# Four-layer graph attention on one core: a planner's rules and durations changed, and layer 3's transfers of half blocks joined

## The chip, the core and the metric

The kernel runs on one core of a Trainium2 chip. What counts is device time in microseconds, from the first to the last instruction of one launch; the runs before gave 2981.0, 2978.83 and 2983.35, median 2981.0. The core has five engines that run their own instruction streams: TensorE (PE in the profile; its weight loads are PEld), VectorE (DVE), ScalarE (ACT), GpSimd (POOL) and SyncE (SP), which here issues nearly all DMA transfers.

## What is computed

128 graphs of 64 nodes, 512 features each, go through four attention layers with a residual. Each layer normalizes, applies a ReLU, attends over the nodes that the adjacency allows, and adds the result to its input:

```python
# layers 0 to 3
h = jnp.maximum(_layernorm(x, axis=-1), 0.0)
x = x + _Ll_gnn_ref(h, adj, ...)

# layers 0 and 2: 4 heads of 64
q, k, v = split_heads(x @ Wq), split_heads(x @ Wk), split_heads(x @ Wv)
sim = jnp.where(adjacency_mask[:, None], jnp.einsum('bhid,bhjd->bhij', q, k) * scale, neg)
out = jnp.einsum('bhij,bhjd->bhid', jax.nn.softmax(sim, axis=-1), v)
return out.transpose(0, 2, 1, 3).reshape(B, N, INNER) @ Wo + bo

# layer 1: the same with 8 heads, and a layernorm of its own (gamma, beta) ahead of w_qkv

# layer 3: 8 heads of 64
m = embs @ map_w.T + map_b
n = sem / norm                                  # m by heads, each row over its length
cos_adj = einsum('bhsd,bhtd->bhst', n, n) * (~sm) > 0.1
q, k = m @ q_w.T + q_b, m @ k_w.T + k_b         # by heads
p_attn = softmax(where(sm, NEG, q k^T / 8)) * keep
adj = cos_adj * p_attn
Ax = einsum('hbst,hbtd->hbsd', adj, embs @ gcn_map_w.T + gcn_map_b)   # by heads
out = relu((Ax @ gcn_W.T) / (adj.sum(-1) + 1.0))
```

Everything is in float32.

## The kernel before

The 8192 rows are cut into 16 groups of 512 rows (`TB` = 4 blocks of 128 rows, two graphs each). A step (l, s) is layer l on group s; 64 steps run through, layer by layer, and neighbouring steps overlap.

**A step.** `loads` brings the group's rows in (xin, two transfers of 512 KB, issued on SP); `layernorms` takes statistics on VectorE (L390, L392), a power on POOL (L397), one more small operation on VectorE (L399) and the normalization with ReLU on ScalarE (L406). `transposes` turns the rows by TensorE into ptr (L477; L454 in layer 1) and copies them with ScalarE to hT (L482). The projections follow; then `front` makes the scores (L824, PSUM tile sc), masks them (L835), takes the maximum (L840), subtracts (L843), exponentiates on ScalarE (L846), sums (L849), inverts (L851) and scales on POOL (L853, tile E). `attention` transposes E (L864, copied by L868 to pt), multiplies with v (L983, tile po), and projects back with a residual that `residuals` has loaded to xres; `store` writes the rows to HBM, where the next layer reads them. In layer 3 `last` multiplies E with the values (L1118, tile po3, two blocks of 128 rows per transposed E), `finish` divides, adds the residual (L1029 to L1040) and writes to the output (L1047); `last_residuals` has loaded the residual (L1019).

**A projection** is a Strassen-Winograd product (`winograd`): seven products of halves in place of eight, with sums of the operands made beforehand (`sums_of_b`: L326 on POOL, L323 on VectorE; `sums_of_a` for the weights). The products are named by their PSUM banks: mA, mB, mA (with a sum of the inputs, t), mC, mA, mC, mA. Each product of a bank that still holds something unread must wait until this has been read. The readers are the methods of `Out`: `first` copies with ScalarE (L529, or L533 with a bias), `second` adds on VectorE from PSUM (L542), `add` copies with ScalarE to a spare quarter (L549) and then adds on VectorE (L553), `alone` copies the last product (1, 0) into that same quarter. `Residual` (layers 0 to 2's projections back) copies with ScalarE to u (L924) and adds on POOL (L929). v in layers 0 and 2 is a plain product (L659, bank mmv, copied by L651). PSUM banks: sc one (shared by sc, po and po3), mA two, mm two (mB, mC, mmv, mmn), ptr and ptp two.

**What sets the order.** Nothing is left to a scheduler of the compiler: each engine's instructions stand in the order in which this program emits them, and each engine works through its own in that order, waiting where data are missing. The order comes from a planner in the program. Every loop above is a generator (a stream) that yields an engine, a duration and a latency ahead of each instruction; `Order.run` keeps a clock for each engine and always lets the stream go on whose next instruction could start first; at equal starts the lower priority number wins. The readers of PSUM have number 0, `fronts` 1, `attentions` 2, `transposes` 3, `weights`, `loads` and `layernorms` 4, projections 5. A load is planned with 0.35 us on SP and 2.2 us until it has landed. `Event` is a wait within the plan; the waits on the chip are made by the tile framework from what each instruction reads and writes. `Ring` and `Bank` hand out buffers and make a stream wait in the plan until an older buffer is given back.

Of the kernel before, what the change touches and what calls it, by code (L numbers as in the profile page):

```python
# [43 lines left out]

class Event:
# [38 lines left out]


class Order:


    def __init__(self):
        self.live, self.free, self.now, self.held = [], {}, 0.0, set()  # L90

# [28 lines left out]

    def run(self):
        while self.live:
            new = [s for s in self.live if s.op is None]
            if new:
                self.step(new[0])
                continue
            s = min(self.live, key=lambda s: (s.start(self.free), s.prio))
            eng, dur, lat = s.op
            at = s.start(self.free)
            self.free[eng] = at + dur  # L130
            s.ready = at + dur + lat
            s.last = (eng, at + dur)
            self.step(s)
        assert not self.held, [where(s.gen) for s in self.held]
# [51 lines left out]

def dve(us):
    return ("dve", us, 0.1)
# [10 lines left out]
def load(us=2.2):  # L199
    return ("sp", 0.35, us)  # L200
# [3 lines left out]
def gnn_stack(ctx: ExitStack, tc: tile.TileContext, a: dict, out: bass.AP):  # L204
# [111 lines left out]
    def sums_of_b(B, T, vector=False):  # L316

        n = T.shape[2]
        for o, i0, i1 in ((T[:, 0], B(0, 1), B(0, 0)), (T[:, 1], B(1, 1), T[:, 0]),
                          (T[:, 2], B(1, 1), B(0, 1)), (T[:, 3], B(1, 0), T[:, 1])):  # L320
            if vector:
                yield dve(0.6 * n)
                nc.vector.tensor_tensor(o, i0, i1, ALU.subtract)  # L323
            else:
                yield pool(0.65 * n)
                nc.gpsimd.tensor_tensor(o, i0, i1, ALU.subtract)  # L326
# [57 lines left out]
    def scales(v):  # L384
# [13 lines left out]
        yield dve(0.2)  # L398
# [4 lines left out]
    def normalize(v, rs, func):  # L403
        for t in range(2):
            yield act(0.69)
# [11 lines left out]
    def loads(steps):  # L417
        for l, s in steps:
            if l > 0:
                yield x_done[l - 1, s]  # L420
            for half in range(2):
                v, e = yield from r_xin.new()
                loaded[l, s, half] = v, e
                yield load()
# [94 lines left out]
    class Out:  # L519
# [5 lines left out]
        def first(self, i, k, p_, read, done):  # L525
# [4 lines left out]
            else:  # L530
                for m in range(2):
                    yield act(0.45)
# [12 lines left out]
        def add(self, i, k, p_, after, read, done):  # L545
# [6 lines left out]
            yield dve(0.7)  # L552
# [3 lines left out]
        def alone(self, i, k, p_, done):  # L556
            yield from self.first(i, k, p_, done, od.event())

    def winograd(A, BT, tokens_out, out_, used, begun):

        B, T, *sums = BT

# [3 lines left out]
        def first(i, k, p_):  # L566
            read, done = ev(2)
            od.spawn(out_.first(i, k, p_, read, done), 0)
            return read, done

        def second(i, k, p_, after):
            done = od.event()
            od.spawn(out_.second(i, k, p_, after, done), 0)
            return done

        def add(i, k, p_, after):
            read, done = ev(2)
            od.spawn(out_.add(i, k, p_, after, read, done), 0)
            return read, done
# [26 lines left out]
        od.spawn(out_.alone(1, 0, p_, pe_), 0)  # L606
        od.spawn(when([c11, c12, c22, pe_], used), 0)
# [152 lines left out]
    def norms(mT, s, m_ready, ready, used):  # L760
# [30 lines left out]
        for c in range(NC):  # L791
            t, e = yield from r_u.new("nr")
            yield ("sp", 0.35, 1.0)
# [15 lines left out]
    def scores(lT, rT, npair, blocks):  # L809
# [3 lines left out]
        for b, t in enumerate(blocks):  # L813
            for ch in range(nch):
                j = ch * nb + b
                yield pe(0.29)
# [55 lines left out]
    def masks(l, s):  # L872
# [3 lines left out]
        yield load()  # L876
# [22 lines left out]
    def residuals(l, s, w_there, got):  # L899
        yield w_there  # L900
        for k in range(2):
            xr, xe = yield from r_xres.new()
            yield load()
# [8 lines left out]
    class Residual(Out):  # L912
# [26 lines left out]
        def alone(self, i, k, p_, done):  # L939
            return self.second(i, k, p_, None, done)  # L940

    def store(l, s, done, got, evs):
# [3 lines left out]
        for k in range(2):  # L946
            xr, xe = got[k]
            yield load()
# [10 lines left out]
    def attention(l, s):  # L959
# [8 lines left out]
        for u, blocks in enumerate(units):  # L968
# [3 lines left out]
            for b, t in enumerate(blocks):  # L972
                for ch in range(nch):
                    j = ch * per + b
                    yield pe(0.29)
# [32 lines left out]
    def last_residuals(s, got):  # L1008
        for t in range(TB):
            if t % 2 == 0:  # L1010
                v2, e2 = yield from r_xres.new()
            v = v2[:, t % 2, :]
            e = e2 if t % 2 else None
            xr = v.rearrange("p (g e) -> p g e", g=2)
            for s2 in range(2):
                for g in range(2):
                    ch = s2 ^ g
                    yield load()
                    nc.sync.dma_start(  # L1019
                        xr[s2 * N:(s2 + 1) * N, g, :],  # L1020
                        x_of(3, s)[t * P + g * N:t * P + (g + 1) * N, ch * 256:(ch + 1) * 256])
            got[t] = (v, xr, e)
            got["e", t].set()

    def finish(s, t, po, poe, got):
# [17 lines left out]
        for s2 in range(2):  # L1043
            for g in range(2):
                ch = s2 ^ g
                yield load()
                nc.sync.dma_start(out[row + g * N:row + (g + 1) * N, ch * 256:(ch + 1) * 256],  # L1047
                                  xr[s2 * N:(s2 + 1) * N, g, :])
# [48 lines left out]
    def last(s):  # L1097
# [3 lines left out]
        for u in range(2):  # L1101
# [3 lines left out]
            for b, t in enumerate(blocks):  # L1105

                po, poe = yield from r_sc.new("po3")
                for i in range(4):
                    yield pe(0.15)
# [90 lines left out]
```

## Time and profile before

The profiled execution took 2978.9 us on the core, at a granted TensorE clock of 0.996.

| | busy us | share of the span | instructions |
|---|---|---|---|
| TensorE, products | 2910.6 | 98% | 27176 |
| TensorE, weight loads | 2468.1 | 83% | 27176 |
| VectorE | 1727.3 | 58% | 2748 |
| POOL | 1465.2 | 49% | 1144 |
| ScalarE | 1336.6 | 45% | 2361 |

A product of 128 x 256 floats is two instructions in the profile, whose starts are about 0.216 us apart when nothing is missing (eight of them take some 1.73 us). By layer, from the busy time in stretches: layer 0 ends near 490 us, layer 1 near 1440, layer 2 near 1960, and layer 3's last step lies behind 2900. DMA is busy at 24.3% on the queue of SP.

In a line of the waits there stand: the waiting engine, tile and line, the releaser, the idle time in total, how many times, and the longest. In a line of the timeline: start and duration in us, engine, line, operation, output and input, shapes, how many, and in brackets the idle time of the engine before it and what ended it.

### The profile page before, as it was taken

The numbers are of one execution on the slowest core, as the hardware profiler recorded it, in microseconds if no ns is written. First come the engines' busy times: TensorE is split into PE (matmuls) and PEld (weight loads), VectorE is DVE, ScalarE is ACT, GpSimd is POOL, SyncE is SP. The second block draws the span as 40 slices with busy tenths as digits, with TensorE's granted clock in tenths as the row PEclk, the third lists the DMA queues.
The fourth block names the chain that finished last, engine by engine and source line by source line (L and its number), as shares of the span: only waits on it lengthen the run. The fifth ranks groups of instructions, "written<-read, shape, count | busy, mean of one in ns | idle before, by whom it ended". The sixth has DMA issues, their size and how long they took to land.

```text
span 2978.9 us, 63888 instructions
## 1 busy us (share of the span) xinstructions
PE 2910.6 (98%) x27176; PEld 2468.1 (83%) x27176; DVE 1727.3 (58%) x2748; ACT 1336.6 (45%) x2361; POOL 1465.2 (49%) x1144
## 2 busy tenths in 40 slices
PE   8999999999999999999999999999999999999997
PEld 6888888888888888888888888887888787888876
DVE  5665566664554555445456556556666666665566
ACT  4444445544444444433444444454444444444442
POOL 6666667444344334335566566663344343344332
PEclk9999999999999999999999999999999999999998
DMA  5323333211112112113233332422232222222212
GB/s 163 116 88 123 95 101 126 67 62 66 48 45 73 59 44 73 59 44 98 94 114 104 102 116 88 138 82 64 72 90 83 63 62 66 70 85 71 52 48 62
DMA packets 162957, 244.05 MB, mean 82 GB/s; under 512 B 17392, under 2 KB 69616, under 8 KB 162672
## 3 DMA queue, kind: packets, MB, share of 16 engines
q1 hardware_dynamic: 149760, 226.56, 24.3%
q10 hardware_dynamic: 12912, 13.42, 1.4%
q8 instruction: 213, 3.49, 0.5%
q14 instruction: 72, 0.59, 0.1%
HBM read 168.60 MB, written 71.30 MB: 81 GB/s over the span
## 4 chain that ended last, share of the span: by engine, by line
PE 85%; DVE 6%; ACT 4%; DMA 2%; POOL 2%; issue 1%; SPq 0%; DVEq 0%; ACTq 0%; POOLq 0%
PE mA L516 37%; PE mC L516 18%; PE mB L516 10%; PE sc L824 4%; PE mmv L659 4%; PE ptp L864 3%; PE ptr L477 3%; PE po L983 2%; ACT E L846 1%; PE po L1118 1%; DVE E L843 1%; DVE sc L835 1%; DVE mx L840 1%; PE mmn L773 1%; PE ptr L454 1%
## 5 line engine op out<-in xcount | busy, mean ns | idle before, releaser
L853 POOL TENSOR_TENSOR E<-E,sm 128x1024 f32<-128x1024 f32 x96 | 186.3, 1941 | 424.2 <-DVE sm L851 298.7
L390 DVE BATCH_NORM_STATS2 st<-xin 128x6 f32<-128x512 f32 x320 | 215.6, 674 | 260.2 <-DMA xin<-x 206.9
L929 POOL TENSOR_TENSOR xres<-xres,u 128x512 f32<-128x512 f32 x192 | 243.4, 1268 | 250.0 <-ACT u L924 245.0
L908 POOL TENSOR_TENSOR xres<-xres,u 128x512 f32<-128x512 f32 x192 | 257.7, 1365 | 219.5 <-DMA xres<-x 99.6
L406 ACT ACTIVATE xin<-xin,rs 128x512 f32<-128x512 f32 x320 | 243.7, 808 | 110.9 <-DVE rs L399 110.7
L397 POOL TENSOR_TENSOR rs<-rs,mhalf 128x2 f32<-128x2 f32 x160 | 118.4, 740 | 276.9 <-DVE rs L395 270.3
L659 PE MATMUL mmv<-w_vo,hT 128*128 128x256 f32 x1024 | 233.4, 380 | 0.9 <-DVE xres L542 0.9
L659 PEld LDWEIGHTS mmv<-w_vo,hT 128*128 128x128 f32 x1024 | 193.5, 190 | 29.0 <-DVE xres L542 2.6
L326 POOL TENSOR_TENSOR t<-hT 128x512 f32<-128x512 f32 x128 | 178.3, 1393 | 73.2 <-ACT hT L482 39.0
L326 POOL TENSOR_TENSOR t<-hT,t 128x512 f32<-128x512 f32 x128 | 172.3, 1346 | 50.5 <-ACT hT L459 46.6
L399 DVE SCALAR_TENSOR_TENSOR rs<-mv,rs 128x2 f32<-128x2 f32 x160 | 80.3, 502 | 197.7 <-POOL rs L397 197.7
L516 PE MATMUL mA<-t,w_qk 128*128 128x256 f32 x768 | 187.0, 380 | 2.8 <-ACT qk L529 2.5
L516 PE MATMUL mA<-t,w_k 128*128 128x256 f32 x768 | 182.7, 381 | 4.8 <-ACT kT L533 4.7
L516 PE MATMUL mA<-t,w_q 128*128 128x256 f32 x768 | 187.1, 379 | 0.0
L516 PEld LDWEIGHTS mA<-t,w_k 128*128 128x128 f32 x768 | 144.8, 190 | 28.2 <-ACT kT L533 8.3
L516 PEld LDWEIGHTS mA<-t,w_qk 128*128 128x128 f32 x768 | 143.1, 190 | 22.0 <-ACT qk L529 3.3
L868 ACT COPY pt<-ptp 128x512 f32<-128x512 f32 x192 | 112.7, 588 | 105.1 <-PE ptp L864 105.1
L516 PEld LDWEIGHTS mA<-t,w_q 128*128 128x128 f32 x768 | 143.1, 190 | 18.1
L849 DVE TENSOR_REDUCE sm<-E 128x16 f32<-128x1024 f32 x96 | 116.4, 1212 | 69.5 <-ACT E L846 69.5
L757 POOL TENSOR_TENSOR v<-v,gcn_row 128x512 f32<-128x512 f32 x64 | 81.4, 1305 | 150.4 <-ACT v L615 150.4
L482 ACT COPY hT<-ptr 128x512 f32<-128x512 f32 x192 | 113.7, 592 | 74.1 <-PE ptr L477 74.1
L846 ACT ACTIVATE E<-E 128x1024 f32<-128x1024 f32 x96 | 101.5, 1058 | 83.6 <-DVE E L843 83.3
(210 smaller groups left out, 6819.0 us busy)
## 6 DMA issues: line engine op xcount, KB each, us to landing
x<-xres SPq DMA_DIRECT2D x96, 512.0 KB, 3.8
xin<-x SPq DMA_DIRECT2D x96, 512.0 KB, 3.8
xres<-x SPq DMA_DIRECT2D x64, 512.0 KB, 4.2
xin<-in_x SPq DMA_DIRECT2D x32, 512.0 KB, 3.8
xres<-in_x SPq DMA_DIRECT2D x32, 512.0 KB, 4.6
u<-rs SPq DMA_DIRECT2D x128, 128.0 KB, 3.1
xres<-x SPq DMA_DIRECT2D x256, 64.0 KB, 2.3
out<-xres SPq DMA_DIRECT2D x256, 64.0 KB, 2.1
```

Of the source, the lines that this page charges most:

```text
L326: nc.gpsimd.tensor_tensor(o, i0, i1, ALU.subtract)
L390: nc.vector.bn_stats(st, v[:, t, :])
L397: nc.gpsimd.tensor_tensor(rs[:, 0, :], rs[:, 1, :], mhalf[:, :2], ALU.pow)
L406: nc.scalar.activation(v[:, t, :], v[:, t, :], func, bias=rs[:, 2, t:t + 1], scale=rs[:, 0, t:t + 1])
L516: nc.tensor.matmul(o, l, r, start=(first and m == 0 and k == 0), stop=(k == KC - 1), skip_group_check=True)
L659: nc.tensor.matmul(p_[:, 0:n], inT[:, c, t * P:(t + 1) * P], w[:, c, :], start=(c == 0), stop=(c == NC - 1))
L824: nc.tensor.matmul(S[a_ * N:(a_ + 1) * N, par, col], lT[r, c, k], rT[r, c, k], start=True, stop=True)
L846: nc.scalar.activation(E, E, AF.Exp, scale=0.125)
L849: nc.vector.tensor_reduce(sm, E, AX.X, ALU.add)
L853: nc.gpsimd.tensor_mul(E, E, sm[:, :, None].to_broadcast([P, 16, N]))
L908: nc.gpsimd.tensor_add(xr[:, t, :], xr[:, t, :], bo[l])
L929: nc.gpsimd.tensor_add(v, v, both(u))
```

## The change

Three things are changed. First, the planner: `urgent` looks, before an instruction of ScalarE or VectorE with a number above 0 is emitted, whether a stream with number 0 could start on that engine before that instruction would end (less 0.1 us), and emits this one instead. Second, durations in the plan: a switch between products on quarters of the array (`quads`: scores, po, po3) and others counts 0.085 us, and loads, normalization, sums and some others have new numbers. In `winograd`, `alone` waits in the plan until the quarter it writes has been added (c22), and `used` is set after every reader instead of after the last ones. Third, layer 3's residuals and outputs go in two transfers of 64 x 2 x 256 floats for each block of 128 rows, where it were four of 64 x 256; `by_half` builds the pattern of addresses in HBM.

```diff
+DRAIN = 0.085
...
+    def quads(self):
+        return self.op[3:] == ("quads",)
...
+    def urgent(self, s):
+
+        eng, end = s.op[0], s.start(self.free) + s.op[1] - 0.1
+        if s.prio <= 0 or eng not in ('act', 'dve'):
+            return None
+        r = [x for x in self.live if x.prio <= 0 and x.op is not None and x.op[0] == eng
+             and x.start(self.free) < end]
+        return min(r, key=lambda x: x.start(self.free), default=None)
...
             s = min(self.live, key=lambda s: (s.start(self.free), s.prio))
-            eng, dur, lat = s.op
+            s = self.urgent(s) or s
+            eng, dur, lat = s.op[:3]
             at = s.start(self.free)
+            if eng == "pe":
+                at += DRAIN * (self.quads != s.quads())
+                self.quads = s.quads()
...
 def load(us=2.2):
-    return ("sp", 0.35, us)
+    return ("sp", 0.6, us)
...
-                yield dve(0.6 * n)
+                yield dve(0.9)
...
-                yield pool(0.65 * n)
+                yield pool(1.42)
...
-        yield dve(0.2)
+        yield dve(0.45)
...
-            yield act(0.69)
+            yield act(0.81)
...
-                yield load()
+                yield load(3.9)
...
-            yield dve(0.7)
+            yield dve(0.92)
...
-        def alone(self, i, k, p_, done):
+        def alone(self, i, k, p_, after, done):
+            yield after
             yield from self.first(i, k, p_, done, od.event())
...
-        od.spawn(out_.alone(1, 0, p_, pe_), 0)
-        od.spawn(when([c11, c12, c22, pe_], used), 0)
+        od.spawn(out_.alone(1, 0, p_, c22, pe_), 0)
+        od.spawn(when([*every, pe_], used), 0)
...
-            yield ("sp", 0.35, 1.0)
+            yield ("sp", 1.3, 3.1)
...
-                yield pe(0.29)
+                yield quads(0.235)
...
-            yield load()
+            yield load(4.6)
...
     def last_residuals(s, got):
-        for t in range(TB):
-            if t % 2 == 0:
-                v2, e2 = yield from r_xres.new()
...
-            for s2 in range(2):
-                for g in range(2):
-                    ch = s2 ^ g
-                    yield load()
-                    nc.sync.dma_start(
-                        xr[s2 * N:(s2 + 1) * N, g, :],
-                        x_of(3, s)[t * P + g * N:t * P + (g + 1) * N, ch * 256:(ch + 1) * 256])
...
+        for t in range(0, TB, 2):
+            v2, e2 = yield from r_xres.new()
+            x3 = v2.rearrange("p t (g e) -> p t g e", g=2)
+            for b in range(2):
+                for s2 in range(2):
+                    yield load(2.3)
+                    nc.sync.dma_start(x3[s2 * N:(s2 + 1) * N, b],
+                                      by_half(x_of(3, s), (t + b) * P, s2))
...
+    def by_half(x, row, s2):
+
+        v = x[row:row + N, s2 * H:(s2 + 1) * H]
+        return bass.AP(tensor=v.tensor, offset=v.offset,
+                       ap=[[D, N], [N * D + (-H if s2 else H), 2], [1, H]])
...
         for s2 in range(2):
-            for g in range(2):
-                ch = s2 ^ g
-                yield load()
-                nc.sync.dma_start(out[row + g * N:row + (g + 1) * N, ch * 256:(ch + 1) * 256],
-                                  xr[s2 * N:(s2 + 1) * N, g, :])
+            yield load(2.3)
+            nc.sync.dma_start(by_half(out, row, s2), xr[s2 * N:(s2 + 1) * N])
```

## The prediction

> **What bounds the kernel now.** I read the page first: TensorE is busy almost without a break, and the chain that ended last is made of its products.
>
> ```profile
> PE 2910.6 (98%) x27176; PEld 2468.1 (83%) x27176; DVE 1727.3 (58%) x2748; ACT 1336.6 (45%) x2361; POOL 1465.2 (49%) x1144
> ...
> PE 85%; DVE 6%; ACT 4%; DMA 2%; POOL 2%; issue 1%; SPq 0%; DVEq 0%; ACTq 0%; POOLq 0%
> ```
>
> The change neither adds nor drops a product, so at the same clock (0.996) it can win only what TensorE idles: 2978.9 - 2910.6 = 68.3 us, 2.3% of the span. The second view is the list of TensorE's waits by releaser; its first nine lines hold nearly all of that.
>
> ```profile
> PE ptr L477 <- ACT xin L406: 12.9, 3, 9.7
> PE mC L516 <- ACT m L533: 8.6, 15, 0.6
> PE mC L516 <- ACT u L924: 6.2, 16, 0.5
> PE po L1118 <- DVE y L1034: 5.4, 3, 2.3
> PE po L1118 <- ACT pt L868: 5.4, 2, 5.2
> PE mmf L363 <- DVE xres L542: 4.7, 1, 4.7
> PE mA L516 <- ACT kT L533: 4.7, 4, 1.2
> PE mA L516 <- ACT qk L529: 2.5, 2, 1.4
> PE mA L516 <- ACT v L529: 1.9, 1, 1.9
> ```
>
> Nearly every line is a product that waits until ScalarE or VectorE has read its PSUM bank. Cut by layer (windows at 490, 1440, 1960 and 2900 us) the same view gives about 21 us for layer 0 (9.7 of them the first load), 4 for layer 1, 7.5 for layer 2, 16 for layer 3 and 13 for the last 79 us. Two stretches of the timeline show why. In layer 0 the Exp (L846) stands on ScalarE ahead of the copies that free the bank of mC:
>
> ```profile
> 251.68 1.06 ACT L846 ACTIVATE E<-E 128x1024 f32<-128x1024 f32 x1 [1.46 <-DVE E L843]
> 252.64 0.35 ACT L651 COPY v<-mmv 128x256 f32<-128x256 f32 x1
> 252.89 0.59 ACT L924 COPY u<-mC 128x512 f32<-128x512 f32 x1
> ...
> 253.53 1.13 PE L516 MATMUL mC<-w_vo,m 128*128 128x256 f32 x4 [0.27 <-ACT u L924]
> ```
>
> In layer 3 VectorE waits for a load (L390), behind it the addition L553, behind that on ScalarE the last copy of qT, then the first of kT, and behind this TensorE:
>
> ```profile
> 2617.20 0.69 DVE L390 BATCH_NORM_STATS2 st<-xin 128x6 f32<-128x512 f32 x1 [4.81 <-DMA xin<-x]
> ...
> 2617.81 1.34 DVE L553 TENSOR_TENSOR qT<-qT 128x512 f32<-128x512 f32 x1
> ...
> 2619.25 0.84 ACT L533 ACTIVATE qT<-mA,vecs 128x256 f32<-128x256 f32 x2 [5.79 <-DVE qT L553]
> ...
> 2620.87 1.99 PE L516 MATMUL mA<-t,w_k 128*128 128x256 f32 x8 [1.17 <-ACT kT L533]
> ```
>
> [...] through the 4.7 us of mmf no later product starts. So where a product stands decides what its wait holds up. [...] the built programs change between 64-row and 128-row products 505 times each, before and after: no gain. [...] The 32 loads here at L781 and L846 take 1283 ns, and Exp follows at once (load at 2890.30, Exp at 2891.59)[...].
>
> **The change, part by part.** I compared the order in which both built programs stand on each engine; instruction counts are equal everywhere but on SP (1042 before, 786 after).
>
> *Readers of PSUM first* (`urgent`). In layers 0 and 2 the Exp stands just ahead of the copy of mC in 31 of 32 steps before; after, in 2, and behind the copies in 28. The copy takes 0.59 us and the product in between, four passes on mA, spaces the two mC products by about 0.86 us: so much is hidden, and the wait of 4.2 (layer 0) + 2.0 (layer 2) = 6.2 us goes. I take -6.2; ends -3 and -10 (the view leaves out gaps under 0.15 us). VectorE's read of mB now precedes the masking copy (L835, 1.23 us): -0.9 us, the wait of mmv on it. In layer 3 the Exp with its table load (1.28 + 1.06 us) still stands ahead of the copy of mC in 15 of 16 steps, as before: the 8.6 us stay.
>
> *Measured durations and `alone` after c22.* The load of xin counts 3.9 + 0.6 us in the plan, in place of 2.2 + 0.35; it landed after 5.2 us in the stretch above. In 11 of layer 3's 16 steps bn_stats stood directly ahead of qT's L553; after, in none: work on po3 comes between, and SP issues the load right behind the stores of the second po3 block, some 8 us of products before bn_stats, so 5 us of landing are hidden. The new wait of `alone` holds only its own copy back in the plan; on the chip that copy already waited for L553 (same tile), so it costs nothing. I take the whole 4.7 us of kT; ends 0 and -6. Of the single waits at the start of layer 0 (2.5) and of layer 3 (2.3 of y) I take -2 together; ends +3 and -5, as the order there changes without a pattern. The 9.7 us of the first load and mmf stay: around mmf both programs have the same order, and it waits for a store and a reload.
>
> *Events of `used`.* A tile is given back in the plan when its last addition is planned, not earlier. That moves emissions, adds no instruction, and the tile framework had these waits anyway: 0.
>
> *Layer 3's transfers.* 512 issues of 64 KB (median 0.595 us each on SP, 2.3 and 2.1 us to landing) become 256 of 128 KB. If one of 128 KB costs the same issue, SP is relieved of 256 x 0.595 = 152 us, none on TensorE's path: the residuals are read many products ahead. Only at the end is a store exposed: the last addition starts at 2973.39 and takes 0.69, four issues follow, the last at 2976.0. Two fewer save 2 x 0.6 = 1.2 us. A transfer of 128 KB may land later: another of that size, the row vectors u<-rs, takes 3.1 us against 2.1. So between -1.2 and +0.1; I take -1.
>
> *What the new order costs.* Work that no product waits for directly is pushed back. The tightest such chain is in layers 0 and 2: Exp, sum (1.20), reciprocal (0.25), scaling on POOL (1.90), then TensorE's transposes.
>
> ```profile
> 256.13 1.90 POOL L853 TENSOR_TENSOR E<-E,sm 128x1024 f32<-128x1024 f32 x1
> ...
> 259.68 0.60 PE L864 MATMUL ptp<-ident,E 128*128 128x128 f32 x4
> ```
>
> Before, it had 259.68 - 258.03 = 1.65 us to spare. With Exp behind both copies (end about 253.9), it ends at 253.9 + 1.06 + 1.2 + 0.25 + 1.9 = 258.3, and with gaps of about 0.1 between engines near 258.4; the transposes come 0.27 earlier, at 259.4. So 1.0 us is left and nothing is lost, if POOL is free at 256.5: of its residual additions (1.27 each) the two ahead end by 255.4. In layer 3 sem's products are no longer interleaved with q's, which brings the two po3 products of a block to 1.7 us apart; the bank is freed in about 1.3 (0.17 + 0.20 + 0.69 and hops). For plans now packed closer to the truth I put +2 us of small waits; ends 0 and +20 (0.6 us in each of 32 steps).
>
> Sum: -6.2 - 0.9 - 4.7 - 2 - 1 + 2 = -12.8 us against the profiled span of 2978.9, so 2966. The three runs have a median of 2981.0, 2.1 above that span: 2981.0 - 12.8 = 2968.
>
> **The rivals.**
> *The waits only move.* Copies come earlier, yet the waits turn up at the next product; ScalarE and VectorE are held idle for readers that come later than planned. For it: waits of 0.3 to 0.6 us come from ordering within a product, and the plan omits table loads. Against it: at 45% and 58% both engines have room. Time: the parts above at about zero, 2975 to 2987, middle 2981. Chance 0.19.
> *The softmax chain becomes the bound* (the slower side). Place: POOL's scaling ahead of the transposes in layers 0 and 2, 32 steps. Its margin falls to 1.0 us by my sum; it decides once the chain slips more than about 1.6 us, as each 0.1 us beyond the margin costs 3.2 us. A slip of 1.7, one POOL addition of 1.3 in the way and a little more, gives 0.7 x 32 = 22, less 12.8: +10, so 2991. For it: POOL is busy 314 of 490 us in layer 0. Against it: the additions ahead of it have their data in time. Chance 0.09.
> *More goes than I count.* The single waits at the layers' seams and the short gaps go too: -25 us, 2956 or less. The 68 us bound it; without first load, mmf, mC of map and the tail's 10 us about 35 are open. Chance 0.12.
> That the transfers aren't halved is excluded by the count on SP.
>
> **How the numbers follow.** Forecast 2968 with chance 0.60 (2957 to 2975 by its own bounds). Below 2955 I leave some 0.09 of the third rival and of the bounds, above 2984 some 0.10, so the range is 2955 to 2984. About 0.2% (6 us) is what a measurement of this kernel can tell from no change. Faster by more: 0.60 + 0.12 = 0.72; within: 0.19; slower: 0.09.
>
> **What would show it.** Right: the lines of mC <- ACT u and mA <- ACT kT gone from TensorE's waits, mC <- ACT m still near 8.6, mmf near 4.7, the last out issues two fewer. Wrong: new lines of ptp or po3 behind POOL, pt or y that repeat 16 or 32 times, or a busy time of TensorE that moves by more than 5 us.

## The result and the profile after

The changed kernel takes 2969.24 us (median of 4 runs, 2967.39 to 2970.03) where the kernel before takes 2980.59 (4 runs, 2978.83 to 2983.35): a ratio of 0.996, 95% interval 0.9943 to 0.9977, or 11.4 us less. The profiled execution took 2967.7 us at the same clock of 0.996, 11.2 less than the one before.

The busy times on the page of the changed kernel:

```profile
PE 2894.8 (98%) x27176; PEld 2465.2 (83%) x27176; DVE 1755.2 (59%) x2748; ACT 1347.4 (45%) x2361; POOL 1470.5 (50%) x1144
```

TensorE's busy time fell by 15.8 us (2910.6 to 2894.8), with the same 27176 instructions. Its idle time rose: 2967.7 - 2894.8 = 72.9 us against 68.3. So the gain is not made of waits that went. The list of TensorE's waits by releaser, changed kernel (total us, times, longest):

```profile
PE ptr L501 <- ACT xin L430: 17.8, 2, 9.4
PE ptp L894 <- DVE E L1120: 15.7, 15, 1.2
PE mC L540 <- ACT m L557: 8.6, 15, 0.6
...
PE mmf L387 <- DVE xres L566: 4.1, 1, 4.1
PE po L1147 <- DVE y L1066: 2.5, 2, 1.4
PE mA L540 <- ACT kT L573: 1.5, 1, 1.5
```

(The lines moved: L516, L824, L864, L1085, L1091, L1118, L773 and L785 of before are now L540, L854, L894, L1114, L1120, L1147, L803 and L815.) The waits of mC on u (6.2 us before) and of mmv are gone, kT fell from 4.7 to 1.5, y from 5.4 to 2.5, qk and v nearly went: with the smaller ones some 20 us. In their place stand three things: ptp on E, 15.7 us where it was 0.5; the start, ptr 17.8 where it was 12.9; and the end, where from the last addition's start to the end it takes 7.5 us (2960.17 to 2967.7) where it took 5.5. With two single waits that are new or longer, by 1.1 us (po on E) and 1.4 us (mmf on bb), these bring some 24.5 us.

**Where the busy time went.** The groups of instructions by shape, norm products (mmn), before and then after; behind the bar is their busy time in us:

```profile
L773 PE MATMUL mmn<-u,sel 128*32 128x512 f32 x128 | 32.8, 605 | 0.0
```

```profile
L803 PE MATMUL mmn<-u,sel 128*32 128x512 f32 x128 | 19.3, 605 | 0.0
```

These 64 products (two instructions each) explain 13.5 of the 15.8 us. The timeline of TensorE in layer 3, before and then after, says why:

```profile
2715.13 1.04 PE L773 MATMUL mmn<-u,sel 128*32 128x512 f32 x2
2716.11 0.66 PE L864 MATMUL ptp<-ident,E 128*128 128x128 f32 x4
2716.69 1.06 PE L773 MATMUL mmn<-u,sel 128*32 128x512 f32 x6
```

```profile
2257.36 0.60 PE L894 MATMUL ptp<-ident,E 128*128 128x128 f32 x4
2257.89 1.07 PE L803 MATMUL mmn<-u,sel 128*32 128x512 f32 x8
```

One product alone takes 1.04 us, three take 1.06, four take 1.07. Each is on 32 columns of the array (128*32 in the lines), and by these times four of them run side by side, if nothing stands between them. Before, transposes stood between the first and the other three in 15 of 16 steps: 31 separate runs. After, there are 18. About 1.05 us for each run gives 32.6 and 18.9.

**The new wait of ptp.** Timeline of layer 3, changed kernel:

```profile
2269.79 1.16 PE L854 MATMUL sc<-m 64*64 64x64 f32 x64
...
2269.83 2.56 DVE L815 RECIPROCAL u<-u 128x128 f32<-128x128 f32 x3
...
2272.31 1.16 DVE L1114 SCALAR_TENSOR_TENSOR Cf<-sc,n 128x1024 uint8<-128x1024 f32 x1
...
2273.58 2.04 DVE L1120 TENSOR_TENSOR E<-E,Cf 128x1024 f32<-128x1024 f32 x1
...
2275.76 0.63 PE L894 MATMUL ptp<-ident,E 128*128 128x128 f32 x4 [1.19 <-DVE E L1120]
```

Three reciprocals of the next step's norms run on VectorE between the scores of m and Cf, the comparison that reads these scores. The scores end at 2270.95; Cf starts 1.36 us later, and the transposes wait 1.19 us. This comes in 13 steps. The other two of the line's 15 waits (0.31 and 0.17 us, near the end) are those that the kernel before has too. Its line, and this stretch of one of its steps:

```profile
PE ptp L864 <- DVE E L1091: 0.5, 2, 0.3
```

```profile
2726.96 1.76 DVE L785 RECIPROCAL u<-u 128x128 f32<-128x128 f32 x2
2727.73 1.16 PE L824 MATMUL sc<-m 64*64 64x64 f32 x64
...
2729.62 0.69 DVE L542 TENSOR_TENSOR qT<-mB,qT 128x512 f32<-128x512 f32 x1 [0.91 <-PE mB L516]
2730.23 1.22 DVE L1085 SCALAR_TENSOR_TENSOR Cf<-sc,n 128x1024 uint8<-128x1024 f32 x1
2731.55 1.23 DVE L1091 TENSOR_TENSOR E<-E,Cf 128x1024 f32<-128x1024 f32 x1
...
2733.24 0.60 PE L864 MATMUL ptp<-ident,E 128*128 128x128 f32 x4
```

There the reciprocals stand ahead of Cf as well, but they are done before the scores are (2728.89); yet Cf starts 1.34 us after the scores, behind an addition to qT. So Cf is not later than it was. Two other things are new, in all 13 steps: E*Cf takes 2.04 us in place of 1.23, and TensorE reaches the transposes 3.62 us after the scores in place of 4.35. E was ready 0.46 us before it was needed, and now comes 1.03 us after. When E*Cf starts, POOL is at an addition to v (L787) in the changed kernel and idle in the kernel before. That this makes E*Cf longer is not shown: no run moves POOL's additions, and at 2938.44 us in the changed kernel E*Cf takes 1.23 us with an addition to v beside it for 1.07 us.

**The start.** Timelines of POOL and TensorE, changed kernel and then the kernel before. In the changed kernel POOL has four sums of the first weight matrix ahead of the second power of the layernorm:

```profile
12.82 5.16 POOL L338 TENSOR_TENSOR w_qk<-w_qk 128x512 f32<-128x512 f32 x4 [4.52 <-DMA w_qk<-in_Wk]
17.94 0.71 POOL L421 TENSOR_TENSOR rs<-rs,mhalf 128x2 f32<-128x2 f32 x1
...
19.74 1.97 PE L501 MATMUL ptr<-ident,xin 128*128 128x128 f32 x8 [8.38 <-ACT xin L430]
```

```profile
10.68 0.69 POOL L397 TENSOR_TENSOR rs<-rs,mhalf 128x2 f32<-128x2 f32 x1 [2.09 <-DVE rs L395]
...
13.04 1.97 PE L477 MATMUL ptr<-ident,xin 128*128 128x128 f32 x8 [1.39 <-ACT xin L406]
```

**The transfers.** The page's DMA issues after (size, median us to landing), and from the waits of SP's queue the line on its own stores:

```profile
xres<-x SPq DMA_DIRECT2D x128, 128.0 KB, 2.7
out<-xres SPq DMA_DIRECT2D x128, 128.0 KB, 2.4
```

```profile
SPq L1077 <- DMA out<-xres: 138.0, 64, 3.4
```

The issue of 128 KB takes 0.604 us (median), that of 64 KB took 0.594, and landing takes 0.3 to 0.4 us more. But SP now stands still 64 times, 2.2 us each, until the first store of a block has landed, before it issues the second. The kernel before has no such line for L1047.

### The profile page after: what moved, and what is told of

It reads as the page before. It is cut to its first block, busy times and chain, and to the rows that moved or that the text cites. A ratio compares the mean times of both kernels' runs of the same rounds, so it can differ in the third digit from the quotient of the medians.

```text
span 2967.7 us, 63784 instructions
## 1 busy us (share of the span) xinstructions
PE 2894.8 (98%) x27176; PEld 2465.2 (83%) x27176; DVE 1755.2 (59%) x2748; ACT 1347.4 (45%) x2361; POOL 1470.5 (50%) x1144
## 4 chain that ended last, share of the span: by engine, by line
PE 87%; DVE 8%; ACT 3%; POOL 1%; issue 1%; DMA 1%; SPq 0%; DVEq 0%; POOLq 0%; ACTq 0%
PE mA L540 37%; PE mC L540 18%; PE mB L540 10%; PE mmv L689 7%; PE sc L854 4%; PE ptp L894 3%; PE ptr L501 3%; PE po L1013 2%; PE po L1147 1%; DVE u L815 1%; DVE E L1120 1%; DVE v L666 1%; PE ptr L478 1%; ACT m L557 1%; DVE y L1066 1%
## 5 line engine op out<-in xcount | busy, mean ns | idle before, releaser
L959 POOL TENSOR_TENSOR xres<-xres,u 128x512 f32<-128x512 f32 x192 | 263.3, 1373 | 169.6 <-ACT u L954 123.8
L938 POOL TENSOR_TENSOR xres<-xres,u 128x512 f32<-128x512 f32 x192 | 267.2, 1412 | 81.5 <-DMA xres<-x 45.9
L430 ACT ACTIVATE xin<-xin,rs 128x512 f32<-128x512 f32 x320 | 252.6, 814 | 43.0 <-DVE rs L423 42.6
L350 POOL TENSOR_TENSOR t<-hT 128x512 f32<-128x512 f32 x128 | 170.1, 1329 | 190.7 <-ACT hT L506 176.1
L414 DVE BATCH_NORM_STATS2 st<-xin 128x6 f32<-128x512 f32 x320 | 214.6, 670 | 24.6 <-ACT xin L430 12.9
L540 PE MATMUL mA<-t,w_q 128*128 128x256 f32 x768 | 192.4, 382 | 0.0
L540 PE MATMUL mA<-t,w_qk 128*128 128x256 f32 x768 | 187.3, 379 | 0.0
L540 PE MATMUL mA<-t,w_k 128*128 128x256 f32 x768 | 182.0, 379 | 1.5 <-ACT kT L573 1.5
L898 ACT COPY pt<-ptp 128x512 f32<-128x512 f32 x192 | 112.7, 587 | 114.7 <-PE ptp L894 114.5
L540 PEld LDWEIGHTS mA<-t,w_k 128*128 128x128 f32 x768 | 145.5, 190 | 21.6 <-ACT kT L573 1.9
L540 PEld LDWEIGHTS mA<-t,w_qk 128*128 128x128 f32 x768 | 143.1, 190 | 18.1
L954 ACT COPY u<-mA 128x512 f32<-128x512 f32 x144 | 84.4, 586 | 159.1 <-PE mA L540 155.6
L540 PEld LDWEIGHTS mA<-t,w_q 128*128 128x128 f32 x768 | 140.2, 190 | 17.4
L501 PE MATMUL ptr<-ident,xin 128*128 128x128 f32 x768 | 119.6, 279 | 17.8 <-ACT xin L430 17.8
L894 PE MATMUL ptp<-ident,E 128*128 128x128 f32 x768 | 118.7, 278 | 16.4 <-DVE E L1120 15.7
```

What stands on the lines that cost most here:

```text
L414: nc.vector.bn_stats(st, v[:, t, :])
L430: nc.scalar.activation(v[:, t, :], v[:, t, :], func, bias=rs[:, 2, t:t + 1], scale=rs[:, 0, t:t + 1])
L501: nc.tensor.transpose(pt[:, c, :], x[:, t, c * P:(c + 1) * P], ident)
L540: nc.tensor.matmul(o, l, r, start=(first and m == 0 and k == 0), stop=(k == KC - 1), skip_group_check=True)
L894: nc.tensor.transpose(pt[:, j, :], Ev[:, par * 4 + j, :], ident)
L938: nc.gpsimd.tensor_add(xr[:, t, :], xr[:, t, :], bo[l])
```

## The experiments

Each batch of runs had its own runs of the kernel before beside it (medians 2982.0, 2983.1, 2985.3 and 2983.9 us); the ratio to these is what is compared.

**The norm products alone.** In the kernel before, the four products are emitted in one go:

```diff
+        yield pe(0.96)
         for c in range(NC):
-            yield pe(0.24)
             nc.tensor.matmul(p_[32 * c:32 * (c + 1), :], sel, sqs[c][0], start=True, stop=True)
```

> The kernel before, with one edit: the four products mmn of the norms (32 columns each) are emitted in one go, so that nothing stands between them on TensorE. Everything else in the plan keeps its place. Theory A (the gain of the change comes largely from mmn, whose four products run side by side only when they follow each other): mmn's busy time falls from 32.8 us to about 19, TensorE's idle stays near 68, and the kernel gains 10 to 14 us, as much as the whole change. Theory B (the gain comes from waits for the readers of PSUM): no change, within 3 us.

Measured: 2968.09 us (6 runs, 2959.61 to 2971.17), ratio 0.995, 0.9939 to 0.9961. The group by shape and the page's first line of this kernel:

```profile
L773 PE MATMUL mmn<-u,sel 128*32 128x512 f32 x128 | 17.7, 605 | 0.0
```

```profile
PE 2892.9 (98%) x27176; PEld 2465.4 (83%) x27176; DVE 1732.1 (59%) x2748; ACT 1335.6 (45%) x2361; POOL 1468.4 (50%) x1144
```

Moving one line in the code gains 13.9 us by the medians, as much as the whole change. The norm products lose 15.1 us of busy time; the waits on u and m stay (4.8 and 8.6 us). The execution that was profiled is the fastest of the six (2959.61 us). Its span is 21.1 us shorter than that of the kernel before: 17.7 us of busy time, and 3.4 us of idle time, since kT waits 1.2 us in place of 4.7, although VectorE's order is the same. So the kT line differs between executions by itself.

**The reciprocals.** In the changed kernel each reciprocal works on 8 of its 128 columns, which leaves most of the norms out of the result; the plan and every place in the order stay.

```diff
-            nc.vector.reciprocal(v, v)
+            nc.vector.reciprocal(v[:, 0:8], v[:, 0:8])
```

> The changed kernel, with the four reciprocals of the norms (L815) cut to 8 of their 128 columns each while the plan and the order stay as they are; most of the norms are left out of the result that way. Theory A (the new wait of ptp for E in layer 3, 15.7 us, comes from three reciprocals of 0.87 us that stand on VectorE ahead of the comparison Cf): the wait falls to under 3 us and the kernel gains 12 to 17 us over the changed one, to about 2954. Theory B (E's multiplication is late because VectorE is slowed by POOL, or because E is late from POOL): at least half of the wait stays, 2961 to 2969.

Measured: 2955.69 us (4 runs, 2952.92 to 2959.24), ratio 0.9912, 0.9899 to 0.9925: by the medians 13.5 us less than the changed kernel. The wait of ptp on E is what it was in the kernel before:

```profile
PE ptp L894 <- DVE E L1120: 0.5, 2, 0.3
```

So the wait goes when nothing keeps Cf after the scores, and nearly its whole length is time of the kernel. The reciprocals are a sufficient handle on it, not its only cause: E*Cf still takes 2.11 us in the 13 steps. E is ready 3.51 us after the scores there, just ahead of the transposes (3.62).

**Outputs in four stores again**, the rest of the changed kernel kept:

```diff
-            nc.sync.dma_start(by_half(out, row, s2), xr[s2 * N:(s2 + 1) * N])
+            for g in range(2):
+                ch = s2 ^ g
+                nc.sync.dma_start(out[row + g * N:row + (g + 1) * N, ch * 256:(ch + 1) * 256],
+                                  xr[s2 * N:(s2 + 1) * N, g, :])
```

> The changed kernel with the outputs of layer 3 in four transfers of 64 KB again, residuals still in two of 128 KB, and the plan as in the changed kernel. Theory A (the second store of a block waits on SP until the first has landed, because the framework takes the interleaved address patterns for overlapping): the waits vanish, SP issues four stores back to back in about 2.5 us where two took 2.4 + 0.6, and from the start of the last addition to the end of the span it is 5.5 us as before and not 7.5; the kernel gains 1 to 3 us. Theory B (a store of 128 KB simply lands later): the same 1 us at the end, but the start of a second store never waits for the first one in the changed kernel.

Measured: 2966.97 us (4 runs, 2965.72 to 2967.39), ratio 0.9949, 0.9936 to 0.9961. Its interval overlaps that of the changed kernel, so the time alone does not settle 2.3 us. The traces do, in part: SP's line of waits on its own stores is gone, and the end takes 6.2 us in place of 7.5.

**The transfers in the kernel before.** Both of layer 3's transfers joined, order and plan as before (the joined transfer is planned as the two that it replaces):

```diff
-                for g in range(2):
-                    ch = s2 ^ g
-                    yield load()
-                    nc.sync.dma_start(xr[s2 * N:(s2 + 1) * N, g, :], ...)
+                yield load()
+                yield load()
+                nc.sync.dma_start(xr[s2 * N:(s2 + 1) * N], by_half(x_of(3, s), t * P, s2))
...
+            nc.sync.dma_start(by_half(out, row, s2), xr[s2 * N:(s2 + 1) * N])
```

> The kernel before with residuals and outputs of layer 3 in two transfers per block, and the plan of before (two planned issues for each transfer): the transfer part of the change alone. By the prediction: -1.2 to +0.1 us. Theory A (second stores wait for the first): 1 to 3 us slower, nearly all of it at the end, since nothing on TensorE waits for a store; TensorE's waits stay as before up to the last step.

Measured: 2999.72 us (4 runs, 2993.52 to 3000.81), ratio 1.0052, 1.0038 to 1.0067. Neither the prediction nor theory A had expected 18 us. Timeline of layer 3 in this kernel:

```profile
2110.36 8.89 SPq L1049 DMA_DIRECT2D out<-xres  x4
...
2119.34 0.55 SPq L425 DMA_DIRECT2D xin<-x  x1
...
2123.85 0.69 DVE L390 BATCH_NORM_STATS2 st<-xin 128x6 f32<-128x512 f32 x1 [4.84 <-DMA xin<-x]
...
2127.70 0.68 DVE L553 TENSOR_TENSOR kT<-kT 128x512 f32<-128x512 f32 x1
...
2129.74 1.28 PE L824 MATMUL sc<-kT,qT 64*64 64x64 f32 x48 [0.99 <-ACT kT L533]
```

Four stores hold SP for 8.89 us (eight took 5.43 in the kernel before at the same place), because two of them wait for landings. The load of xin behind them goes out late, VectorE waits for it, and the addition to kT stands behind VectorE's wait. Set beside the kernel before product by product, this kernel loses 10.6 us in layer 3, in small steps in most of the 16 groups. The other 8 us of the profiled execution come mostly at two places in layers 0 and 2 (near 50 and 1470 us), which the edit does not touch; their cause stays open. At the second place the kernel of the counter-test that follows, in which no store waits, loses 2.7 us as well.

The counter-test joins the residuals only and leaves the outputs in four:

> The kernel before with layer 3's residuals read in two transfers per block, and its outputs written in four as before; the plan is as before. The kernel before with both joined had taken 2999.7 where 2982 was the base. Theory A (the loss came from the second store of each block, which waits on SP for the landing of the first and holds the next loads of xin back): the time is that of the kernel before within 4 us, 2978 to 2986, no store waits for a landing, and sc<-ACT kT is not in the list of TensorE's waits. Rival B (joined transfers land later or disturb other transfers by their size): still over 2990.

Measured: 2984.19 us (12 runs, 2980.08 to 2992.3), ratio 1.0003, 0.9994 to 1.0012. No store waits for a landing, and the line sc <- ACT kT is gone. So the loss comes with the joined stores, not with the joined residuals. No run joins the stores without the wait, so the wait and the size of a store are not told apart by time alone.

**Without the rule for readers of PSUM**, the changed kernel otherwise:

```diff
             s = min(self.live, key=lambda s: (s.start(self.free), s.prio))
-            s = self.urgent(s) or s
```

> The changed kernel without the rule that lets readers of PSUM go first; durations, events and transfers of the changed kernel stay. The work is the same, only the order differs. In it the Exp again stands ahead of the copy of mC in layers 0 and 2, and in layer 3 three of the four reciprocals of the norms stand behind the multiplication E*Cf where the changed kernel has three ahead of Cf. Theory A (the rule is what took away the waits of mC on u, and what put the reciprocals ahead and so made the new wait of ptp in layer 3): mC<-ACT u comes back with about 6 us, ptp<-DVE E falls from 15.7 to under 2, kT stays small; the sum is about 8 us faster than the changed kernel, some 2961. Rival B (the forecast's reading: the rule is the larger part of the gain, and the order it leaves costs nothing): 6 to 8 us slower than the changed kernel, some 2976. Rival C (the place of the reciprocals is due to the durations): ptp stays near 15 and the time is about 2975.

Measured: 3007.74 us (4 runs, 3006.27 to 3011.54), ratio 1.008, 1.0063 to 1.0097. No theory came near. The wait of ptp did fall to 0.5 us, as theory A had it, but mC on u came back with only 1.3 us, though the Exp stands ahead of the copy again. Instead kT waits, 38.6 us (TensorE's waits, then a stretch of the timeline; line numbers are one lower than in the changed kernel, L539 is its L540):

```profile
PE mA L539 <- ACT kT L556: 38.6, 10, 5.4
```

```profile
2636.51 1.08 SPq L448 DMA_DIRECT2D xin<-x  x2
...
2638.53 1.89 PE L539 MATMUL mC<-t,w_k 128*128 128x256 f32 x8
2641.31 0.69 DVE L413 BATCH_NORM_STATS2 st<-xin 128x6 f32<-128x512 f32 x1 [8.79 <-DMA xin<-x]
...
2643.13 0.69 DVE L565 TENSOR_TENSOR kT<-mB,kT 128x512 f32<-128x512 f32 x1
...
2645.82 3.78 PE L539 MATMUL mA<-t,w_k 128*128 128x256 f32 x8 [5.39 <-ACT kT L556]
```

Without the rule, bn_stats stands ahead of the addition to kT, and waits 8.79 us for a load that SP had issued late. A second reading: the eight instructions after the wait take 3.78 us, those before it 1.89. Start to start they stand 0.427 us apart in place of 0.216. The granted clock was 0.51 from 2645.8 to 2651.5 us and 1.00 in the 3.5 us after. In the changed kernel it was 0.50 from 1465.15 to 1468.55 us, behind the wait of mmf (4.08 us), with six intervals of 0.427 us. The length of a pause alone does not decide: the six waits for kT of 3.6 to 5.4 us were followed by several instructions at half pace, of three of 3.2 to 3.4 us only one was, four instructions later, while a wait for m of 3.18 us was followed by 13, and in the kernel with outputs in four below one for kT of 2.52 us by five. In this execution 84 such intervals in the projections add 17.6 us, where the changed kernel has 13 (2.7 us).

**With the old durations**, rule, events and transfers kept (the core of the edit):

```diff
-DRAIN = 0.085
+DRAIN = 0.0
...
-    return ("sp", 0.6, us)
+    return ("sp", 0.35, 2.2)
...
-            yield ("sp", 1.3, 3.1)
+            yield ("sp", 0.35, 1.0)
```

> The changed kernel with all durations and latencies of the plan as they were before, and no cost for a switch of tiling; the rule for readers of PSUM, the events and the transfers of the changed kernel stay. The work is the same. Built, it has the norm products four in a row in 16 places, and the Exp behind the copies of mC. Theory A (the joined norm products and the readers first make the gain, and both come with the rule alone; the durations matter only for loads): mmn busy near 18 us, u gone from the waits, kT between 3 and 6 us, and the time within 6 us of the changed kernel's 2969. Rival B (the durations keep the loads ahead of the second stores that wait on SP; without them the queue of SP is late as in the kernel before with joined transfers): kT, sc and mmf wait some 10 to 15 us more, about 2982.

Measured: 2997.28 us (4 runs, 2995.89 to 3005.29), ratio 1.0046, 1.0029 to 1.0063. As expected, the norm products take 18.6 us and the waits on u and kT are gone. The time isn't as theory A had it, and the waits are not those of rival B. TensorE's waits, and VectorE's in layer 3:

```profile
PE ptp L894 <- DVE E L1120: 31.9, 14, 3.5
PE po L1147 <- DVE y L1066: 20.1, 13, 3.5
```

```profile
DVE nz L914 <- DMA adj<-in_adj: 40.6, 14, 5.1
...
DVE st L414 <- DMA xin<-x: 25.2, 12, 2.9
```

A load planned with 2.2 us that lands after 3.6 (adj) or 3.8 (xin) puts its readers on VectorE ahead of Cf and of po3's division, and these stand behind the wait. Over the whole span VectorE waits 206.9 us for xin in the kernel before, 9.3 us in the changed one.

**Are the stores behind both losses?** The two kernels again with outputs in four:

> The changed kernel without the rule for readers of PSUM, and with the outputs of layer 3 in four stores per block as before; durations and events of the changed kernel stay. The work is the same. The kernel without the rule alone had taken 3007.7, with 38.6 us of waits of TensorE on kT, and half pace after them. Theory A (these waits come from SP: the second store waits for the first, the load of xin goes out late, and without the rule bn_stats, which waits for that load, stands ahead of the addition to kT): mA<-ACT kT falls from 38.6 to under 6 us, ptp<-DVE E stays under 2, and the time is 2955 to 2965, below the changed kernel. Rival B (the late loads come from the plan's order without the rule, whatever the stores do): kT stays over 25 us and the time over 2995.

> The changed kernel with all durations of the plan as they were before, and with the outputs of layer 3 in four stores per block as before; the rule for readers of PSUM and the events stay. The work is the same. The kernel with the old durations and joined outputs had taken 2997.3, with 31.9 us of waits of ptp on E and 20.1 of po3 on y, both behind instructions of VectorE that waited for loads. It fills the last field of a table of four kernels with four stores: rule and durations 2967.0, durations alone 2984.7, neither 2984.2 (residuals joined). Theory A (the stores' waits made the loads late; without them the readers of loads find their data): ptp<-DVE E and po<-DVE y together fall from 52 to under 20 us, and the time is 2960 to 2975. Rival B (the short planned latencies of loads alone put their readers too early): the two stay over 35 us together and the time is over 2985.

Measured: without the rule 2984.69 us (12 runs, 2977.14 to 2993.44), ratio 1.0, 0.999 to 1.001; kT still waits 26.0 us. With the old durations 2992.4 us (12 runs, 2986.0 to 3001.69), ratio 1.0033, 1.0021 to 1.0044; ptp on E 28.1 and po on y 20.2 us. So rival B is nearer in both, though the first time lies between the two theories: by the medians the stores make up 23 us of the first loss, and hardly 5 of the second, where the intervals overlap. The ratios together:

| | outputs in two | outputs in four |
|---|---|---|
| rule and durations | 0.996 | 0.9949 |
| durations, no rule | 1.008 | 1.0000 |
| rule, old durations | 1.0046 | 1.0033 |
| neither (and no events) | 1.0052 | 1.0003 |

Neither part gains alone, although each of them brings the norm products together (18 and 16 runs in place of 31). The waits suggest why. Without the rule, readers of loads stand ahead of the readers of PSUM; with too short latencies, the rule's order meets loads that have not landed. Together the loads come early enough, and kT's additions stand ahead of what waits for them. No run takes back the latencies of the loads alone, or the events alone.

**The start.** The sums of the first weight matrix wait in the plan for the first normalization:

```diff
+            if key == "qk0":
+                yield n_ready[0, 0, 1]
             yield from sums_of_a(o_part(t) if key in ("vo0", "vo2") else t)
```

> The changed kernel with one event more in the plan: the sums of the first weight matrix (four additions on POOL, 5.2 us) are emitted after the normalization of the first group, so that the power of the layernorm does not stand behind them on POOL. The work is the same. Theory A (the second wait of ptr at the start, 8.4 us against 1.4 before, comes from these four additions): ptr<-ACT xin falls from 17.8 to about 11 to 13 us, and the time by 4 to 7 us, to some 2964. Rival B (the first transposes only wait later, for the sums that the first product needs): ptr falls, a wait of mA on POOL of the same size appears, and the time stays at 2969.

Measured: 2966.79 us (4 runs, 2965.86 to 2967.82), ratio 0.9938, 0.9924 to 0.9953; ptr waits 14.3 us. The profiled span is 3.2 us shorter than that of the changed kernel. The second wait fell from 8.38 to 1.39 us, but a third of 3.4 us came with the next group, where a power again stands behind two sums. That is about half of what was expected; by the intervals of the runs alone it is not told from no change.

**All four edits**, nothing left out of the work: the start, outputs in four, norm products in one go, and the reciprocals planned after the last E*Cf of the step before.

```diff
+        if s:
+            yield c_done[s - 1]
         for h in range(4):
             v = rs[:, h * P:(h + 1) * P]
             yield dve(0.87)
...
+            if u == len(units) - 1:
+                c_done[s].set()
```

> The changed kernel with four edits, all of the work kept: the reciprocals of the norms are planned only after the last multiplication E*Cf of the step before; the outputs go in four stores; the sums of the first weight matrix wait in the plan for the first normalization; the four norm products are emitted in one go. Theory A (each edit takes what the runs of it alone or the trace showed: reciprocals 13 to 15 us, stores 2.3, start 2.4, norm products 19.3 to 17.7, so 1.6): 2969 less 20, some 2949, with ptp<-DVE E under 3 us and mmn near 17.7. Rival B (the reciprocals put behind make the scaling of m by them late, or take the place of what stood there): a wait of the same size at m, sc or qT, and the time near 2963.

Measured: 2954.49 us (4 runs, 2951.97 to 2954.55), ratio 0.9893, 0.9877 to 0.991. That is faster than both kernels: 14.7 us less than the changed one by the medians, and some 20 us by the ratios to the kernel before (0.9893 against 0.996), whose median was 4.7 us higher in this batch. TensorE's waits and the timeline of layer 3 (L898 and L1127 are the changed kernel's L894 and L1120):

```profile
PE ptr L503 <- ACT xin L432: 14.2, 3, 9.5
...
PE ptp L898 <- DVE E L1127: 6.4, 15, 0.5
```

```profile
2261.79 1.16 PE L858 MATMUL sc<-m 64*64 64x64 f32 x64
2263.01 1.22 DVE L1121 SCALAR_TENSOR_TENSOR Cf<-sc,n 128x1024 uint8<-128x1024 f32 x1 [1.12 <-PE sc L858]
...
2264.34 2.11 DVE L1127 TENSOR_TENSOR E<-E,Cf 128x1024 f32<-128x1024 f32 x1
2266.38 1.75 DVE L819 RECIPROCAL u<-u 128x128 f32<-128x128 f32 x2
...
2266.60 0.63 PE L898 MATMUL ptp<-ident,E 128*128 128x128 f32 x4 [0.47 <-DVE E L1127]
```

By the profile the edits bring 9.3 (ptp), 3.6 (ptr), 1.6 (mmn) and 1.5 us (the end, 6.0): 16.0, against a span that is 15.0 shorter. Theory A asked for ptp under 3, but 6.4 stay: E is ready 3.5 us after the scores, as with the short reciprocals, but TensorE reaches the transposes after 3.19 us, since two product instructions fewer stand ahead of them. With E*Cf at the 1.23 us of before, by these figures, E would be in time. Rival B's new waits did not come.

## Why the prediction was right, and where it was not

The total was right: 12.8 us less were predicted, 11.4 came, and 2969.2 lies 1.2 us from 2968. Its composition was not: two misses of about 13 us each cancel (13.5 us of the norm products that were not seen, and some 15 us of new waits where 2 were put). That the number came out is luck. Nor does its upper bound of 2975 follow from the parts: their slow ends, as written, add up to +19 us, or 3000.

- **"It can win only what TensorE idles."** Failed. 15.8 us came out of the busy time, idle time rose by 4.6. A count of waits bounds neither: products that could run side by side and do not (13.5 us here), and products at half pace after a pause (0.427 us apart in place of 0.216; 17.6 us without the rule), both stand in the profile as busy. The reading of the waits was too generous as well: the nine lines that were to hold "nearly all" of the 68.3 us hold 52, and six of them, 29 us, wait for a reader of a bank.
- **"505 times each, before and after: no gain."** This is the step that failed most. It counted the changes between products of 64 and of 128 rows (in the kernel before a score starts 0.30 us after the projection's product ahead of it, where two such products stand 0.216 us apart), and left out the products on 32 columns. Their separate runs fell from 31 to 18, and 13.5 us of busy time with them; the run with that alone gained 13.9.
- **Readers of PSUM first, -6.2 and -0.9.** These waits are gone, as forecast. But the rule is not the only cause: without it u waits 1.3 us, not 6, with the Exp ahead of the copy again. What else in the new order takes that wait away is not separated.
- **kT, -4.7.** It fell by 3.2, within its ends, and of the four places of before, in the middle of layer 3, none is left; the 1.5 us stand at the layer's start. How much of this is the change is not sure, since the line was 1.2 us in the run of the norm products and 3.5 with the residuals joined, both with VectorE's order as before. That the durations would do it alone was wrong: with them and without the rule kT waits 38.6 us (26.0 with the outputs in four). bn_stats still waits for loads, and only the rule puts the additions to kT ahead of it.
- **The single waits, -2.** qk and v fell by some 4.5 us and y by 2.9, more than the step's lower end of 5, but the start took 4.9 back by POOL's weight sums. "The order there changes without a pattern" was a way of not looking: POOL's order at the start showed it. "The 9.7 us of the first load" did stay (9.4).
- **The transfers, -1, between -1.2 and +0.1.** Outside its ends: the end of the kernel became 2.0 us longer. The counts of issues and the landings were about right (2.4 and 2.7 us). That the second store would wait for the first was not seen: SP's queue was priced by issues, not by the waits in it. "None on TensorE's path" holds in the changed order only; in the order before, the kernel with joined stores takes some 18 us more.
- **What the new order costs, +2, ends 0 and +20.** It cost some 15 us, within the ends but at another place. In layers 0 and 2 the chain by POOL's scaling held, as worked out (0.6 us in all on POOL). In layer 3 the chain from the scores of m by Cf and E*Cf to the transposes had 0.46 us to spare. It lost this when E*Cf took 2.04 us in place of 1.23 and the transposes came 0.7 us sooner, with three reciprocals now in the place of the addition to qT. The step looked for the tightest chain where the rule was meant to work, not in each place where the order changes.
- **mC on m (8.6) and mmf** stayed as forecast (8.6 and 4.1), the wait on u went, and that on kT shrank. But signs named as wrong appeared too: a line of ptp that repeats in 13 steps (behind VectorE's E, not behind POOL, pt or y), and a busy time moved by more than 5 us.

Of the rivals, the softmax chain did not become the bound in layers 0 and 2. A mechanism like it, transposes that wait for a chain on VectorE, appeared in layer 3. "More goes than I count" was true of the waits (20 us), and "the waits only move" of the place they left. Not settled are 2.3 us of the busy time beyond the norm products, why E*Cf takes longer, and the two places in layers 0 and 2 named above.

## What to carry to other kernels

Put products on quarters of the columns next to one another, and count their separate runs in the built order: each run cost about 1.05 us here, as much as four products in a row, and showed as busy time, not as a wait. Before a new wait is put down to what stands ahead of it in a queue, look at the same stretch of the kernel before: here Cf started as late there. For a rule that pulls some instructions forward, list in each stage what is pushed back and who waits for that; and time a rule together with the durations it decides by, because here each alone lost time or gained none. Ahead of joining transfers, look at whether the second will wait for the first (here 64 times, 2.2 us each), and what stands behind it in the queue.

## What the runs showed of the hardware

- Four products of 128 x 512 on different quarters of the columns took 1.07 us in a row, one alone took 1.04.
- After a pause, the instructions of products of 128 x 256 came at 0.427 us in place of 0.216, up to 13 in a row. The wait of 5.39 us was followed by twelve such intervals, 12 x 0.21 = 2.5 us on top of its length; one of 3.35 us was followed by none, one of 2.52 us by five. The granted clock stood at 0.51 behind the wait of 5.39 us, and at 0.50 behind one of 4.08 us.
- E*Cf (128 x 1024 on VectorE), the second of a step, took 1.23 us in the kernel before and, in 13 steps, 2.03 to 2.11 in the changed kernel and two of its variants, where POOL's additions to v ran beside it. That the one causes the other is not shown; once it took 1.23 us with such an addition beside it.
- Stores whose addresses interleave were issued one after the other's landing: 64 waits of 2.2 us on SP. That the framework takes them for overlapping is inferred from this; no run tested another pattern of addresses.
